# A perceiver layer on one core: the order of steps that share a stretch is reversed, and the last tiles' timetable is moved

## The chip, the cores and the metric

The kernel runs on one core of a Trainium2 chip. The time is the device time of one execution in microseconds (us); the number given for a kernel is the median of several runs. [...] An instruction that waits holds back everything behind it on its engine.

## The reference

All in float32. The layer has three parts, each with a layer norm ahead of it and a residual sum behind it:

```
x = x + cross_attention(norm(x), ctx, ctx)     # 32 x 64 queries, 32 x 1601 keys, 16 heads of 16
x = x + span_attention(norm(x))                # scores = -softplus(s1) * (pos - 64*sigmoid(s0))^2
x = x + ffn(norm(x))                           # (shared + experts / 2) / 2
shared  = (silu(x @ sw1 + sb1) * (x @ sw3 + sb3)) @ sw2 + sb2
experts = sum over k of gelu(x @ w1[e] + b1[e]) @ w2[e] + b2[e],  e = (11 * token + 7919 * k) % 8
```

The second part's attention runs over the 64 positions of one sequence, and its scores come from two numbers per head and position (s0, s1) alone. All softmaxes are exact ones.

## The kernel before

The 32 sequences are 16 **tiles** of two sequences (128 rows). The first part's attention is the bulk of the work: for each sequence and each half of the heads (64 "halves", `n`), keys and values are projected (`pk`, `pv`, L494), scores are made (`psc`, L548), DVE adds the mask (L572, L565) and keeps running maxima (`mrun`, L589), the maxima are turned over PE (`pm`, `pb`), POOL subtracts them (L620), ACT takes the exponential (L625), and PE multiplies with the values (`pvs`, L635).

A half is three **stretches** (3n, 3n+1, 3n+2). Beside it run short chains of small work, written as Python generators: `query_steps` makes the queries of the next tile (norm, `tr_q`, `pq` L465, `qbd` L473), `finish_steps` ends a sequence's first attention, and `span_steps(t)` does all of the second part for tile t and the norm of the third. Each `yield` names how many stretches later the chain goes on. `agenda` holds, for each stretch, the generators that are due, and `run(stretch)` takes each one step on, in list order, and appends it to the list of a later stretch. The program's order on PE, DVE, ACT and POOL is this written order: a `manual_schedule` keeps it.

The 23 steps of `span_steps` are, by place in the timetable `STEPS` (and the three other ones for the last tiles): 0 output projection `po` (L250), sum into x (L253) and statistics; 1 POOL's norm scalars (L205 to L208); 2 ACT's norm `xn_h` (L214); 3 transpose `tr_h`, copy `hT` (L262); 4 `psp` (L266), DVE `span`, `z` (L272, L273); 5 ACT `z` = exp (L280); 6 some 16 small DVE operations (L293 to L305); 7 POOL `sc` = pos - mean (L310); 8 ACT square (L314), POOL times soft (L315); 9 DVE `least` (L318); 10 to 13 four groups of four exponentials (L322); 14 `pval` (L334), copies `vbd` (L341); 15 DVE reciprocal (L346); 16 POOL weights `sc` (L348); 17 `psa`, copies `aT` (L356, L358); 18 `po2`, copy `o2T` (L366, L372); 19 `po3`, sum, statistics (L376, L379), and the transfer `x_kept` on SP (L381); 20 norm scalars; 21 `xn_f` (L214); 22 `tr_f` and the copies into `xfT` (L221, L389).

A tile's chain starts every 12 stretches and takes 24 to 25, so up to three tiles and a query chain meet in a stretch. Where "stretch 3 of a tile" is said, it is the stretch in which step 0 of that tile runs, counted as `STEPS` counts, modulo 12.

The last tiles (13, 14, 15) have their own timetables. After the last half (stretch 189 on) a loop over s = 2 to 21 calls `run(189 + s)`, then `gate()` as often as `gated` says, then starts the units that `begin` names. A **unit** u is one 128-channel slice of the shared network's hidden layer for a quarter of the tokens: one product with `sw1` and one with `sw3` (L664; for some units the second is made earlier, L672). `gate()` takes the oldest unit begun: ACT's Silu and DVE's product (L686, L687, or L691, L692). Units 12 to 15 need the third norm of tiles 12 to 15. All these products, and the small ones, take PSUM banks in turn from one pool of six (`mm_bank`). The last stage (L914 on) computes the experts and the output.

[...]

Of the kernel before, what the change touches and what calls it, by code (L numbers as in the profile page):

```python
# [89 lines left out]
def perceiver_kernel(ctx: ExitStack, tc: tile.TileContext, a: dict[str, bass.AP], out: bass.AP):  # L90
# [126 lines left out]
    def transposed(src, name: str):  # L217
# [12 lines left out]

    STEPS = (3, 4, 5, 6, 7, 8, 9, 11, 12, 15, 16, 17, 18, 19, 20, 20, 21, 22, 23, 24, 25, 26, 27)
    LAST_BUT_TWO = (
        3, 4, 5, 6, 7, 8, 9, 11, 12, 13, 13, 14, 15, 16, 17, 17, 17, 18, 20, 21, 22, 25, 27,
    )
    LAST_BUT_ONE = (
        2, 2, 3, 4, 5, 5, 6, 7, 8, 9, 10, 11, 12, 13, 14, 14, 14, 15, 16, 17, 17, 18, 19,
    )
    LAST = (2, 2, 3, 4, 5, 6, 8, 9, 10, 11, 12, 12, 12, 12, 13, 13, 13, 15, 16, 17, 17, 18, 19)
    SMALL = 6
# [343 lines left out]
    def maximum(n: int, k: int):  # L583

        dst = mrun
        if k == NKC - 1:
            dst = mxs[n] = work.tile([P, 4, P], F32, tag="mx", bufs=1, name="mx")
        dst, run = (m[:CHUNK].rearrange("p (r i) q -> p r i q", r=2) for m in (dst, mrun))
        nc.vector.tensor_tensor(dst, block_of(n, k), run, ALU.max)  # L589
# [105 lines left out]
    held_at: set = set()  # L695

    def run(stretch: int):
        for steps in agenda.pop(stretch, []):
            while (wait := next(steps, None)) == 0:
                pass  # L700
            if wait:
                agenda[stretch + wait].append(steps)
# [62 lines left out]
    for n, (b, c) in enumerate(halves[:-1]):  # L765
# [9 lines left out]
        def steps(g: int):  # L775
            run(3 * n + g)
            for u in extra.get(3 * n + g, ()):
                linear_factor(u)
# [14 lines left out]
        if not held:  # L793
            first_maxima(n + 1)
        run(3 * n)
        if n:
            values(n - 1, 1)
# [30 lines left out]
    stretch = 3 * last  # L828
# [17 lines left out]
    gate()  # L846


    begin = {4: (1, 2), 7: (7, 8, 5), 10: (9,), 12: (10,), 15: (6, 4), 19: (11,)}
    gated = {7: 2, 10: 2, 12: 1, 13: 1, 15: 1, 17: 2}  # L850
    for s in range(2, 22):
        run(stretch + s)
# [149 lines left out]
```

## Time and profile before

| | |
|---|---|
| median of 3 runs | 1526.94 us (1526.82 to 1529.74) |
| the profiled execution, its own time | 1529.89 us |
| its span, first to last instruction | 1528.1 us |
| steady loop, one tile | some 84 us (`po` at 643.4 and 727.7) |
| tail, last half to the experts' stage | 1374 to 1442 us |
| experts' stage | 1442 us to the end |

An engine's busy time is the time in which it had an instruction at work. In a timeline a line is a group of like instructions: start, time, engine, line and operation, tile written from tiles read, count, and in brackets the idle time ahead of it with what ended it. PE's line is 664 for units, and its clock, as granted, is in the windows view (1.00 is full speed).

### The profile page before, as it was taken

How to read it: one execution, taken by the hardware profiler on the slowest of the kernel's cores; microseconds unless marked ns; L12 is line 12 of the kernel's file. 1: busy time of each engine (PE TensorE's matmuls, PEld its weight loads, DVE VectorE, ACT ScalarE, POOL GpSimd, SP SyncE). 2: the span in 40 equal slices, each digit the busy share in tenths (PEclk: the TensorE clock that was granted, in tenths of full speed). 3: DMA queues.
4: the chain of work that ended last, by engine and by line, in shares of the span. 5: the costliest groups of instructions: out<-in, count | busy, mean ns of one | idle time of the engine just before them, and what ended most of it. 6: DMA issues, size and time to landing. Idle time of an engine off the chain costs nothing.

```text
span 1528.1 us, 62953 instructions
## 1 busy us (share of the span) xinstructions
PE 1470.4 (96%) x28600; PEld 1071.4 (70%) x28600; DVE 1222.8 (80%) x2332; ACT 947.7 (62%) x1727; POOL 1119.0 (73%) x508
## 2 busy tenths in 40 slices
PE   8999999999999999999999999999999999988999
PEld 5677767777777767777776767676777767654587
DVE  4889898988889898989888898888898889873100
ACT  3565657676667657676767666675767676756411
POOL 1777787888878887879878788878788787852610
PEclk9999999999999999999999999999999999999999
DMA  5111111111111101111111111111111111004100
GB/s 173 43 38 46 46 46 46 44 45 49 49 49 50 42 23 46 53 36 49 49 50 49 50 49 32 33 45 53 36 50 49 50 46 32 6 6 159 59 28 29
DMA packets 52076, 73.82 MB, mean 48 GB/s; under 512 B 3812, under 2 KB 51040, under 8 KB 51680
## 3 DMA queue, kind: packets, MB, share of 16 engines
q1 hardware_dynamic: 50992, 69.00, 14.7%
q8 instruction: 225, 3.69, 1.0%
q10 hardware_dynamic: 816, 0.79, 0.2%
q14 instruction: 43, 0.35, 0.1%
HBM read 65.57 MB, written 4.19 MB: 46 GB/s over the span
## 4 chain that ended last, share of the span: by engine, by line
PE 72%; DVE 17%; ACT 8%; issue 2%; POOL 0%; DMA 0%; ACTq 0%; DVEq 0%; POOLq 0%
PE pv L494 18%; PE pk L494 18%; PE psc L548 11%; PE pvs L635 8%; DVE mrun L589 7%; DVE prob L572 6%; PE py L932 4%; ACT sc L322 3%; PE pm L596 2%; ACT prob L625 2%; PE u L664 2%; PE ph L914 2%; PE pb L611 2%; PE pq L465 1%; PE psa L356 1%
## 5 line engine op out<-in xcount | busy, mean ns | idle before, releaser
L620 POOL TENSOR_TENSOR prob<-prob,mb 124x1664 f32<-124x1664 f32 x252 | 937.7, 3745 | 239.4 <-ACT mb L615 231.6
L572 DVE TENSOR_TENSOR prob<-psc,madd 124x512 f32<-124x512 f32 x768 | 506.6, 680 | 70.8 <-PE psc L548 69.2
L625 ACT ACTIVATE prob<-prob 124x1664 f32<-124x1664 f32 x256 | 406.9, 1590 | 181.7 <-POOL prob L620 179.1
L589 DVE TENSOR_TENSOR mrun<-prob,mrun 124x512 f32<-124x512 f32 x704 | 486.1, 691 | 40.7 <-ACT mrun L581 28.0
L494 PE MATMUL pk<-ct,wkT_sb 128*32 128x372 f32 (+1 forms) x2512 | 387.6, 489 | 5.7 <-DMA wkT_sb<-in_wkT 5.6
L494 PE MATMUL pv<-wvT_sb,ct 128*124 128x256 f32 x3524 | 380.9, 379 | 0.4 <-DVE prob L572 0.3
L494 PEld LDWEIGHTS pv<-wvT_sb,ct 128*124 128x124 f32 x3524 | 273.6, 132 | 108.7 <-issue 14.9
L548 PE MATMUL psc<-qbd,kT 32*124 32x128 f32 x6400 | 246.6, 280 | 17.0 <-ACT hT L262 9.7
L494 PEld LDWEIGHTS pk<-ct,wkT_sb 128*32 128x32 f32 (+1 forms) x2512 | 148.9, 127 | 135.9 <-issue 88.9
L548 PEld LDWEIGHTS psc<-qbd,kT 32*124 32x124 f32 x6400 | 204.7, 182 | 54.7 <-issue 19.7
L526 ACT COPY v<-pv 124x512 f32<-124x512 f32 (+1 forms) x224 | 124.4, 556 | 164.0 <-PE pv L494 163.9
L635 PE MATMUL pvs<-prob,v 124*17 124x64 f32 x13312 | 214.3, 220 | 1.2 <-issue 1.2
L635 PEld LDWEIGHTS pvs<-prob,v 124*17 124x17 f32 x13312 | 196.7, 98 | 23.1 <-issue 15.2
L509 ACT ACTIVATE kT<-pk,cols 128x372 f32<-128x372 f32 (+2 forms) x256 | 146.7, 585 | 69.1 <-PE pk L494 69.0
L322 ACT ACTIVATE sc<-sc,least 128x64 f32<-128x64 f32 x256 | 85.7, 339 | 2.8 <-DVE least L318 2.8
L934 DVE SCALAR_TENSOR_TENSOR ot<-py,prob 128x256 f32<-128x256 f32 x16 | 6.8, 424 | 75.7 <-PE py L932 75.7
L581 ACT COPY mrun<-prob 124x512 f32<-124x512 f32 x64 | 38.2, 597 | 41.4 <-DVE soft L305 38.3
L664 PE MATMUL u<-xfT,sw_sb 128*128 128x512 f32 x128 | 61.1, 627 | 0.9 <-ACT xfT L389 0.9
L596 PE MATMUL pm<-cst,mx 124*128 124x124 f32 x256 | 42.1, 285 | 17.0 <-DVE mx L589 14.1
L611 PEld LDWEIGHTS pb<-cst,mc 128*124 128x124 f32 x256 | 29.5, 135 | 36.8 <-DVE mc L603 28.9
L548 PE MATMUL pvs<-qbd,kT 32*124 32x128 f32 x256 | 54.9, 294 | 0.0
L565 DVE TENSOR_TENSOR prob<-psc,madd_fifth 124x256 f32<-124x256 f32 x64 | 27.0, 421 | 32.2 <-PE pvs L548 31.1
(126 smaller groups left out, 1242.4 us busy)
## 6 DMA issues: line engine op xcount, KB each, us to landing
ct<-in_ctxT SPq DMA_DIRECT2D x64, 372.0 KB, 3.2
ct<-in_ctxT SPq DMA_DIRECT2D x32, 496.0 KB, 5.1
ct<-in_ctxT SPq DMA_DIRECT2D x32, 361.0 KB, 4.0
w<-in_w SPq DMA_DIRECT2D x16, 256.0 KB, 7.0
x<-in_x SPq DMA_DIRECT2D x16, 128.0 KB, 2.1
x_kept<-x SPq DMA_DIRECT2D x16, 128.0 KB, 1.8
prob<-x_kept SPq DMA_DIRECT2D x8, 256.0 KB, 5.6
out<-ot SPq DMA_DIRECT2D x16, 128.0 KB, 1.9
```

The lines of the kernel that those rows point to most:

```text
L322: nc.scalar.activation(sc[:, h, :], sc[:, h, :], AF.Exp, bias=least[:, h : h + 1], scale=-1.0, accum_out=total[:, h : h + 1],)
L494: nc.tensor.matmul(out[at:end], lhsT=lhsT[:, at:end], rhs=rhs, start=start, stop=stop, **(dict(tile_position=(0, at)) if tiled else {}),)
L509: nc.scalar.activation(kTs[c][:, k0 : k0 + kn], ps[:, :kn], AF.Identity, bias=cols[:, B_K + c : B_K + c + 1])
L526: nc.scalar.copy(vs[b % 2][:kn, 2 * u : 2 * u + n, :, :DK], ps[:kn, : n * D].rearrange("p (n h d) -> p n h d", n=n, d=DK),)
L548: product = nc.tensor.matmul(ps[:CHUNK, at * P : (at + 1) * P], lhsT=kTs[c][32 * j : 32 * j + 32, k0 : k0 + CHUNK], rhs=qbd[b // 2][32 * j ...
L572: nc.vector.tensor_tensor(pair_of(n, j)[:, c0 : c0 + 4, :].rearrange("p k (e q) -> p k e q", e=2), pss[j][:CHUNK].rearrange("p (k e q) -> ...
L589: nc.vector.tensor_tensor(dst, block_of(n, k), run, ALU.max)
L596: nc.tensor.transpose(ps[:, j * CHUNK : (j + 1) * CHUNK], m[:CHUNK, j, :], ident[:CHUNK, :CHUNK])
L620: engine.tensor_tensor(sj, sj, m[:CHUNK, j, None, :].to_broadcast([CHUNK, NKC, P]), ALU.subtract)
L625: nc.scalar.activation(pair_of(n, j), pair_of(n, j), AF.Exp)
L635: nc.tensor.matmul(pvs[32 * j : 32 * j + DK + 1, c, :, r, :], lhsT=v[:kn, k, 8 * c + h, :], rhs=pair_of(n, h // 2)[:kn, k, (h % 2) * S : ( ...
L664: nc.tensor.matmul(ps, lhsT=w[:, c, hc * P : (hc + 1) * P], rhs=xfT[:, c, :, slot], start=(c == 0), stop=(c == 1),)
```

## The change

Four edits:

```diff
     LAST_BUT_TWO = (
-        3, 4, 5, 6, 7, 8, 9, 11, 12, 13, 13, 14, 15, 16, 17, 17, 17, 18, 20, 21, 22, 25, 27,
+        3, 4, 5, 6, 7, 8, 9, 11, 12, 13, 13, 14, 15, 16, 17, 17, 17, 18, 20, 21, 21, 21, 23,
     )
     LAST_BUT_ONE = (
-        2, 2, 3, 4, 5, 5, 6, 7, 8, 9, 10, 11, 12, 13, 14, 14, 14, 15, 16, 17, 17, 18, 19,
+        2, 2, 3, 4, 5, 5, 6, 7, 8, 9, 10, 10, 10, 10, 12, 12, 12, 13, 14, 15, 15, 16, 17,
     )
...
     def run(stretch: int):
-        for steps in agenda.pop(stretch, []):
+        for steps in reversed(agenda.pop(stretch, [])):
             while (wait := next(steps, None)) == 0:
                 pass
             if wait:
                 agenda[stretch + wait].append(steps)
...
-    begin = {4: (1, 2), 7: (7, 8, 5), 10: (9,), 12: (10,), 15: (6, 4), 19: (11,)}
+    begin = {3: (1, 2), 7: (7, 8, 5), 10: (9,), 12: (10,), 15: (6, 4), 19: (11,)}
```

`run` takes the generators of a stretch from the end of their list. Tile 13 does its norm scalars and `xn_f` in the stretch of `po3`, and its `tr_f` four stretches sooner. Tile 14 does its four groups of exponentials in one stretch, and everything after them two stretches sooner. Units 1 and 2 begin in s = 3 and not in s = 4. No instruction is added or taken away but table loads.

## The prediction

> **What bounds the kernel now.** I read the page's engine shares, then its chain by line, then the tail (1374 us to 1442 us) on the PE and ACT timelines, because the edits to the lists act only there, and last one tile of the steady loop, because `run` is used everywhere.
>
> ```profile
> PE 1470.4 (96%) x28600; PEld 1071.4 (70%) x28600; DVE 1222.8 (80%) x2332; ACT 947.7 (62%) x1727; POOL 1119.0 (73%) x508
> ```
>
> PE is the bound: 1528.1 - 1470.4 = 57.7 us idle in all, so whatever is won or lost is a PE gap. The tail, PE first:
>
> ```profile
> 1379.33 1.10 PE L250 MATMUL po<-woP_sb,oT 128*128 128x256 f32 x4 [1.59 <-DVE oT L718]
> ...
> 1387.61 1.09 PE L356 MATMUL psa<-cst,sc 128*128 128x128 f32 x8 [1.34 <-POOL sc L348]
> ...
> 1390.02 9.98 PE L664 MATMUL u<-xfT,sw_sb 128*128 128x512 f32 x20
> 1399.84 1.03 PE L376 MATMUL po<-woutT_sb,o2T 128*128 128x256 f32 x4
> 1404.02 0.44 PE L221 MATMUL tr_f<-cst,xn_f 128*128 128x128 f32 x2 [3.15 <-ACT xn_f L214]
> 1404.98 8.83 PE L664 MATMUL u<-xfT,sw_sb 128*128 128x512 f32 x16 [0.52 <-ACT xfT L389]
> ...
> 1419.50 1.09 PE L356 MATMUL psa<-cst,sc 128*128 128x128 f32 x8 [1.05 <-POOL sc L348]
> ```
>
> The last column is the gap before the group. Two gaps are waits of tile 14 (1.34, 3.15); the last (1.05) is tile 15, whose weighted `sc` is late. From there to the end tile 15 is the chain, and after 1427.90 PE works without a gap. ACT beside it:
>
> ```profile
> 1393.09 1.28 ACT L280 ACT_TABLE_LOAD   x1
> 1394.39 0.23 ACT L280 ACTIVATE z<-z 128x32 f32<-128x32 f32 x1
> ...
> 1404.49 0.43 ACT L389 COPY xfT<-tr_f 128x128 f32<-128x128 f32 x2 [0.53 <-PE tr_f L221]
> ```
>
> Tile 15's `z` exponential is done at 1394.62, but DVE reaches the small operations only at 1401.92, behind tile 14's sum.
>
> **The reversal in the steady loop.** A reversed list is appended to the next stretch in reversed order, and is reversed again there. So the order of the generators flips in every second stretch only. The built instruction order confirms it: per tile only its stretches 3, 5 and 7 change; POOL keeps its order.
>
> (a) Stretch 3 of a tile: `tr_f` goes ahead of `po`, `least` behind the norms. DVE then does stats_q (0.56 us), and waits for `po`, which is 0.31 us later; its L589 starts 0.6 us later. The cover is DVE's next wait for PE, 1.21 us, and the tightest PE wait on DVE in between (`pv` at 733.12 for the L565 that ends 732.35) has 0.77 us to spare. Cost 0; without the cover 14 x 0.6 = 8.4 us.
> (b) Stretch 5: the norms ahead of the four exponentials. Same instructions, norm scalars ready long before: 0.
> (c) Stretch 7:
>
> ```profile
> 757.79 0.53 PE L266 MATMUL psp<-wspanT_sb,hT 128*128 128x32 f32 x4
> 758.16 1.14 PE L465 MATMUL pq<-xnT,wqT_sb 128*128 128x128 f32 x8
> 759.23 1.15 PE L548 MATMUL psc<-qbd,kT 32*124 32x128 f32 x32
> 760.31 2.67 PE L494 MATMUL pk<-ct,wkT_sb 128*32 128x372 f32 x32
> ...
> 759.81 1.48 ACT L473 ACTIVATE qbd<-pq,bq,own 128x128 f32<-128x128 f32 x4
> ```
>
> `pq` now precedes `psp`, so the six-bank pool hands `pq`'s bank to the first tiled `pk` (L494) where `psp`'s bank stood before; the second `pk` used to get it. That `pk` now waits for the four `qbd` activations, at 760.31. They start 1.10 us after `pq` starts (89.67 to 90.77, where no exponential stands ahead): 757.79 + 1.10 + 1.50 = 760.39, plus 0.05 for the signal = 760.44. **Stall 0.13 us in each of 14 tiles = 1.8 us.** Bounds: 0.05 (the activations are seen as done earlier) to 0.2, so 0.7 to 2.8 us. Behind the waiting `pk` stand the other `pk` and `pv`; everything on PE shifts.
>
> **The tail, in times of the old profile.** Norm of tile 13: POOL has its scalar at 1375.60, so `xn_f` runs 1375.64; the sixteen exponentials start 1376.13 and take 5.31 (1411.71 to 1417.02) to 1381.44. Silu table and u3: 1381.46 + 1.30 = 1382.76, done 1383.45.
> - PE: after `pvs` (1377.64) `tr_f` 0.31, `pval` 1.01, u1 1.72 (four starts 0.43 apart): 1380.68. u2 stands in the bank of u3's first product, so it waits for that Silu until 1383.49. **Gap 2.7.**
> - DVE: the reciprocal now stands behind the gates of u3 and u0: 1384.74. POOL 1385.08 to 1386.98, `psa` 1387.04. **Gap 1.8.** All four exponential groups together win only 0.57 us here.
> - `po` of tile 15 stands behind `psa`: 1387.97 (before: 1379.33). Its norm passes DVE (1.24 after the matmul's start to the aggregate's end at 1390.21), POOL (1.30), ACT at 1391.55. On ACT `o2T` of tile 14 is queued behind that norm: 1392.04 to 1392.41. `po3` 1392.46. **Gap 2.5.**
> - `tr_h`, its copy, `psp`: u7 starts 1394.80. Five half units x 1.72 end at 1403.40; only then `tr_f` of tile 14 (POOL, `x_kept` and the rest of that norm are covered by these 8.6 us).
> - ACT takes the `xfT` copies of `tr_f` **ahead of** `z`: ready 1404.32, table 1.30, `z` at 1405.62 where it was 1394.39. The small operations follow at once: POOL starts `sc` at 1405.90 + 1.64 = 1407.54 (before 1403.56). Square 1409.48, product 1410.62, `least` 1412.55, exponentials 1413.80, and 7.79 as before (1411.71 to 1419.50) to `psa`: 1421.59.
>
> **Tile 15 ends 2.1 us later**, with the order behind it unchanged. u9's second half waits on the new timing of u7's Silu, but `psa` still comes last. Moving `begin` of u1, u2 to 3 buys nothing, since u2 waits.
>
> SP: `x_kept` of tile 14 is moved ahead of six weight loads, which wait with it until about 1394; their first use is after 1455, so 0.
>
> Hand-over to the last stage:
>
> ```profile
> 1440.22 0.69 ACT L691 ACTIVATE prob<-u,cols 128x512 f32<-128x512 f32 x1 [2.75 <-PE u L664]
> ...
> 1441.73 2.10 PE L914 MATMUL ph<-xfT,w 128*128 128x256 f32 x9
> 1442.01 0.75 DVE L692 SCALAR_TENSOR_TENSOR prob<-u,b3twice,prob 128x512 f32<-128x512 f32 x1 [2.68 <-PE u L664]
> ```
>
> The banks rotate differently: the first `ph` now gets the bank of u15's second product (before: u14's first), and waits for that L692, 1442.76 + 0.05. **1.1 us**; nothing covers it.
>
> [...]
>
> [...] Here the clock is halved after windows that were half idle:
>
> ```profile
> 1390.00:1392.00 2.00, 2.00 (x7) 0.95 (x4) 0.00 (x0) 1.82 (x3) 0.00 (x0) 0.50 1.10 348
> ...
> 1406.00:1408.00 2.00, 2.00 (x4) 0.85 (x3) 1.04 (x2) 1.99 (x4) 0.00 (x0) 0.50 0.00 0
> ```
>
> (The 0.50 is the granted clock.) [...] A half-rate stretch lasted 3.4 us and cost at most 1.7 us. I count two on the path: about 1.4 us near u7 (the old 1.2 us there is not in my 1403.40), and about 1.2 us at `psa` to u11, ahead of which PE now idles 3 to 4 us. Bounds 0 to 5; I take 2.6.
>
> **Sum.** 1.8 + 2.1 + 1.1 + 2.6 = +7.6 us. Against the profiled execution (span 1528.1, its own time 1529.9) that is 1537.5; that execution is 2.95 us above the median, near the top of the three runs. Against the median 1526.94 it is 1534.5; I say **1534 us**.
>
> **Rivals.**
> A. No extra half-rate stretch on the path (windows fall kindly): +5.0, 1532. For it: the tail has a 61% busy window (1419.6 to 1423) at full clock. Against: 6.3 us with u2 alone.
> B. The waits cascade: half rate twice in a row after `psa`, and 0.2 per tile: 1.8 + 1.0 + 2.1 + 1.1 + 5 = +11, 1538.
> C. Not slower: PE order decides, not tile 15. If `z` were not held by the copies of `tr_f` (had ACT taken it first), POOL's `sc` would start near 1400 and `psa` would find PE busy. The 1.05 gap and the old 3.15 + 0.52 then go, and the new gaps cost 2.7 + 1.8 + 2.5 + 0.5 against 1.59 + 0.58 + 1.34: -0.7; with hand-over and the loop's 1.8 at their low ends (0 and 0.7) it is 0, 1527. It decides as soon as `z` ends before about 1401. Against: both queues are in order, and the built order puts the copies first.
> D. The change does little of what it says: flips hidden, loop 0, tail +2.1 + 1.1, the clock as before: +3, 1530, at the edge of what counts.
>
> **Chances.** Forecast 0.5, A 0.2, B 0.12, D 0.1, C 0.08. A difference of 0.2% (3.1 us) is about what this kernel's runs can tell from none. Slower by more: all of forecast, A, B and half of D, 0.87; within: half of D and most of C, 0.09; faster 0.04. Range 1529.5 to 1538.5: D's edge to B.
>
> **What would show it.** The `z` exponential behind the `xfT` copies, 11 us later; u2 waiting on L691; `po3` waiting on `o2T`; `psa` of tile 15 2 to 5 us later; a 1.1 us gap before the first L914; 14 gaps before L494 on L473; six table loads after 1374 us instead of eight. I am wrong if PE's idle time after 1374 us is below the old 10 us, or if tile 15's `psa` isn't late.

## The result, and the profile after

The changed kernel takes 1543.4 us (median of 4: 1539.34 to 1546.07) beside 1527.78 us (four runs) for the kernel before: ratio 1.0098, 95% interval 1.0073 to 1.0124. A second set gave 1540.6 us (six runs) against 1529.55 us (27 runs of the kernel before, 1526.32 to 1535.32): 1.0076 (1.0058 to 1.0093), which is 11.6 us. It is slower, as forecast, but by 11.6 us (second set) to 15 us (first set) and not by 7.6, and both times lie above the range, which ends at 1538.5.

The page, PE's row (PE makes the matrix products and PEld loads their weights; DVE and POOL do vector work, ACT activations). PE's idle time is 62.1 us of the span of 1537.5, 4.4 more than before; its busy time grew by 5.0 with the same 28600 products.

```profile
PE 1475.4 (96%) x28600; PEld 1072.2 (70%) x28600; DVE 1222.6 (80%) x2332; ACT 946.1 (62%) x1725; POOL 1118.9 (73%) x508
```

The PE timeline of the tail (start, time, group; in brackets the gap ahead and what ended it):

```profile
1362.02 1.06 PE L596 MATMUL pm<-cst,mx 124*128 124x124 f32 x4 [2.43 <-DVE mx L589]
...
1383.29 1.99 PE L664 MATMUL u<-xfT,sw_sb 128*128 128x512 f32 x4 [2.12 <-ACT prob L691]
1386.89 1.09 PE L356 MATMUL psa<-cst,sc 128*128 128x128 f32 x8 [1.61 <-POOL sc L348]
1387.82 1.03 PE L250 MATMUL po<-woP_sb,oT 128*128 128x256 f32 x4
...
1392.25 1.74 PE L376 MATMUL po<-woutT_sb,o2T 128*128 128x256 f32 x4 [2.83 <-ACT o2T L372]
...
1395.76 10.66 PE L664 MATMUL u<-xfT,sw_sb 128*128 128x512 f32 x20
...
1410.70 5.42 PE L664 MATMUL u<-xfT,sw_sb 128*128 128x512 f32 x12 [1.56 <-ACT prob L691]
...
1424.40 1.97 PE L356 MATMUL psa<-cst,sc 128*128 128x128 f32 x8 [3.64 <-POOL sc L348]
...
1451.06 7.17 PE L914 MATMUL ph<-xfT,w 128*128 128x256 f32 x32 [0.91 <-DVE prob L692]
```

The three predicted waits are there: u2 on the Silu (2.12; forecast 2.7), psa on POOL (1.61; 1.8), po3 on `o2T` (2.83; 2.5). Tile 15's psa is 4.9 us later than before, behind a gap of 3.64. The same group of eight takes 1.97 here, where the granted clock is 0.50, and 1.09 at 1386.89, where it is 1.00. ACT:

```profile
1406.68 0.43 ACT L389 COPY xfT<-tr_f 128x128 f32<-128x128 f32 x2 [8.49 <-PE tr_f L221]
1407.13 1.28 ACT L280 ACT_TABLE_LOAD   x1
1408.42 0.23 ACT L280 ACTIVATE z<-z 128x32 f32<-128x32 f32 x1
```

`z` stands behind the copies, 14 us later than before; ACT has two table loads fewer (1725 instructions, not 1727). In both profiles a load of 1.28 us stands at each turn from Exp to Silu, from Silu to Exp and, once, from Silu to Gelu: after 1374 us eight before, six here. Last, PE's clock in windows that follow the boundaries of the clock itself (window, its length, busy time of PE, PEld, DVE, ACT, POOL, then the granted clock):

```profile
1419.95:1423.36 3.41, 0.81 (x2) 0.00 (x0) 0.25 (x1) 3.38 (x16) 0.91 (x1) 1.00 0.00 0
1423.36:1426.77 3.41, 2.37 (x24) 1.98 (x24) 0.75 (x1) 2.23 (x4) 0.99 (x1) 0.50 0.00 0
1426.77:1430.19 3.42, 2.54 (x28) 1.84 (x21) 1.29 (x2) 1.66 (x4) 0.00 (x0) 0.50 0.00 0
1430.19:1433.60 3.41, 3.41 (x5) 1.43 (x5) 1.03 (x3) 0.53 (x1) 1.62 (x5) 0.50 0.11 38
```

PE works 0.81 of 3.41 us, and three windows follow at half clock: the first two of them have gaps again (1.04 and 0.88 us idle), and only behind the third, which is busy throughout, does the clock come back. From the last half to the last units the clock is halved for 23.9 us (1361.9 to 1368.7, 1392.6 to 1399.5, 1423.4 to 1433.6); before it was 13.7 us.

In this execution the steady loop nets nothing: the last half's pm starts at 1362.02, and in the profile before:

```profile
1362.03 1.06 PE L596 MATMUL pm<-cst,mx 124*128 124x124 f32 x4 [2.43 <-DVE mx L589]
...
1441.73 7.07 PE L914 MATMUL ph<-xfT,w 128*128 128x256 f32 x32
```

So the whole difference of this pair, 9.3 us, lies between the last pm and the first ph (89.04 us; before 79.70). Two things were open: whether the loop's 1.8 us exist, and what the times have beyond the sum.

### The profile page after: what moved, and what is told of

Read it like the earlier page. It is cut to its first block, busy times and chain, and to the rows that moved or that the text cites. A ratio compares the mean times of both kernels' runs of the same rounds, so it can differ in the third digit from the quotient of the medians.

```text
span 1537.5 us, 62954 instructions
## 1 busy us (share of the span) xinstructions
PE 1475.4 (96%) x28600; PEld 1072.2 (70%) x28600; DVE 1222.6 (80%) x2332; ACT 946.1 (62%) x1725; POOL 1118.9 (73%) x508
## 4 chain that ended last, share of the span: by engine, by line
PE 70%; DVE 17%; ACT 9%; issue 2%; POOL 1%; DMA 0%; DVEq 0%; POOLq 0%; ACTq 0%
PE pv L494 18%; PE pk L494 18%; PE psc L548 10%; PE pvs L635 8%; DVE mrun L589 7%; DVE prob L572 6%; PE py L932 4%; ACT sc L322 3%; ACT prob L625 2%; PE u L664 2%; PE pm L596 2%; PE ph L914 2%; PE pb L611 1%; ACT qbd L473 1%; PE po L376 1%
```

## The experiments

Two theories at first. T: the loop pays about what was forecast, and what the sum lacks is half-rate clock in the tail. L: it lies in the loop. Times are medians beside the kernel before in the same set (1528.4 to 1530.1); the ratio is what counts.

**The whole and its two halves.** `again` is the changed kernel. `loop_only` is the old kernel with `agenda.pop(stretch, [])[:: -1 if stretch < 178 else 1]`; `tail_only` is the changed one with `>= 178`.

> The changed kernel once more, for a second profile and more times. Theory T (tail and clock): times spread over 1539 to 1546 again; the last half's pm (L596) starts at about 1362 as before, within 0.7 us, so the loop nets nothing; what an execution has over the +9.4 us of the first profile is more half-rate clock after 1370 us, in steps of 3.4 us at up to 1.7 us lost each. Rival L (loop): the last half's pm starts 3 to 6 us later than 1362 in a slow execution, with the clock after 1370 as in the first profile.

> The old timetables and the old begin; lists reversed only before stretch 178, so that the tail has its old order and 13 tiles of the loop have the new one. My prediction's term: 13 x 0.13 = +1.7 us, 1529.5. Theory T: 0 to +1.7 us, 1527.5 to 1529.5. Rival L: +4 to +7 us, 1532 to 1535.

> The changed kernel with lists reversed only from stretch 178 on, so that the steady loop has its old order. Theory T: nearly all of the loss stays, +12 to +16 us, 1540 to 1544. Rival L: +8 to +10 us, 1536 to 1538.

| | us | ratio (95%) | x 1528.6 us |
|---|---|---|---|
| again | 1540.6 | 1.0076 (1.0058 to 1.0093) | +11.6 |
| loop_only | 1531.61 | 1.0016 (1.0007 to 1.0025) | +2.4 |
| tail_only | 1537.44 | 1.0056 (1.0036 to 1.0076) | +8.6 |

The halves add up to 11.0. L falls; T's loop is at its upper end or a little over. The waits view of `again` for PE (who waited for what: us in all, times, longest) has the forecast wait, in 14 tiles:

```profile
PE pk L494 <- ACT qbd L473: 2.2, 14, 0.2
```

0.16 us each where 0.13 was forecast. `loop_only` has it too (2.2 us, 14 times); no run takes this one wait away alone. A single pair of profiles could not show it: from the second pm to the last but one, seven executions with the old list order in the loop took 1277.6 to 1280.4 us (median 1278.4), thirteen with the reversed one 1279.8 to 1286.4 (1281.5). The first pair were 1279.79 and 1279.77, one high in its group and the other the lowest.

**Swaps in the tail.** One list taken in its old order turns all later ones too, so the tail can be undone from its end: `[:: 1 if stretch == 3 * last + 8 else -1]` (z_first), with 5 (o2T_first) and 4 (po_first) for the 8; `plain_order` has no reversal at all.

> The changed kernel with one swap on ACT: at s = 8 tile 15's z exponential stands ahead of tile 14's xfT copies; nothing else moves. Theory T (z held by the copies makes tile 15 late): z runs at about 1397 instead of 1408, psa of tile 15 finds PE still busy, its 3.6 us gap and the half-rate stretch behind it go: 5 to 9 us less than the changed kernel, 1534 to 1538. Rival P (PE's order and the waits of tile 14 make the loss, tile 15 has slack): at most 2 us less, 1541 to 1543.

> The changed kernel with the list of s = 5 alone taken in its old order, which turns all later stretches of the tail too: on ACT o2T of tile 14 ahead of xn_h of tile 15 and z ahead of the xfT copies, on PE tr_h of tile 15 ahead of po3 of tile 14; psa of tile 14 still ahead of po of tile 15. By the traces tr_h then starts at about 1392.5 and not 1393.8: 1.2 us less than with z alone first, 1536.5 to 1537. If the 2.8 us gap ahead of po3 is paid in full: 2.8 us less, 1535.

> The same with the list of s = 4 in its old order: also po of tile 15 ahead of psa of tile 14 on PE, so that it runs in the gap in which psa waits for POOL, and tile 15's norm starts 2.7 us sooner. The steady loop stays reversed. If this one place of po holds most of the loss: the old-order kernel plus the loop's cost, 1529.5 to 1530.5. If the loss is spread evenly over the swaps: 1533 to 1535.

> The new timetables and the new begin, lists in their old order. Theory T (timetable and reversal share the loss): the loop's 1.8 us and z's hold (2.6 us by the swap) go, u2's, psa's and po3's waits stay: 1535 to 1537. Rival R (the reversal makes the loss, the timetables alone gain): 1526 to 1530.

| | us | ratio (95%) | from the one above |
|---|---|---|---|
| again | 1540.6 | 1.0076 | |
| z_first | 1538.0 | 1.0053 (1.0033 to 1.0073) | -3.5 |
| o2T_first | 1533.65 | 1.0036 (1.0024 to 1.0049) | -2.6 |
| po_first | 1531.19 | 1.0015 (1.0004 to 1.0026) | -3.2 |
| plain_order | 1527.35 | 0.9987 (0.9980 to 0.9995) | -4.3 |

(The last column is the difference of the ratios times 1528.6 us; neighbours' intervals overlap, the ends are clear.) The last step has the loop's 2.4 us in it. No single swap holds the loss; `o2T_first` came out 3 us lower than its traces promised, `po_first` 1 us higher. The swap of z was worth 3.5 us where 5 to 9 were expected, and ACT of `z_first` says why:

```profile
1399.37 0.23 ACT L280 ACTIVATE z<-z 128x32 f32<-128x32 f32 x1
1407.32 0.43 ACT L389 COPY xfT<-tr_f 128x128 f32<-128x128 f32 x2 [7.72 <-PE tr_f L221]
1407.77 1.28 ACT L691 ACT_TABLE_LOAD   x1
1409.07 1.27 ACT L691 ACTIVATE prob<-u,cols 128x512 f32<-128x512 f32 x2
1410.22 1.05 ACT L314 ACTIVATE sc<-sc 128x1024 f32<-128x1024 f32 x1
```

`z` is 9 us earlier, but the square of the same chain (L314) stands behind the same copies and the two Silus after them: it is 2.06 us earlier (1412.28 in the changed kernel), and psa with it. PE still waits 2.47 us for that psa. (This execution, 1533.94 us, is the fastest of its six, and no half rate follows psa in it.) Without any reversal the new timetables are 2.0 us faster than the kernel before (interval 0.8 to 3.1).

**The clock alone.** Products that nobody reads keep PE at work in its gaps:

```diff
+    def filler(n: int):
+        for _ in range(n):
+            nc.tensor.matmul(spare_pvs, lhsT=ident, rhs=woP[:, 0, :], start=True, stop=True)
...
+        filler({14: 6, 15: 1}.get(t, 0))
         for c in range(2):
             nc.tensor.matmul(
                 po3[:, :D], lhsT=o2T[:, c, :], rhs=woutT[:, c, :], start=(c == 0), stop=(c == 1)
```

> The kernel before, with products that nobody reads put into PE's gaps from the last half on (10 ahead of and behind pm, then 5, 4, 11, 3 and 3 ahead of po of tile 15, psa of tile 14, tr_f of tile 14, psa and po3 of tile 15; each 0.26 us at full clock, just under the gap in sum). Theory T (short PE gaps halve the clock, and that is paid in time): no half-rate stretch after 1360 us, 3 to 5 us less than before, 1525 to 1526.5 against 1529.6. Rival N (the half rate falls where PE would wait anyway): within 1 us of before.

> The changed kernel, filled in the same way (7 ahead of u2, 5 ahead of psa of tile 14, 10 ahead of its po3, 5 ahead of u9's second product, 11 and 2 ahead of psa and po3 of tile 15, 10 around the last pm). Theory T (what my sum lacks is half-rate clock): no half-rate stretch after 1360 us, 6 to 9 us less than the changed kernel, 1532 to 1535; and against the filled kernel before the waits alone stay, +5 us as in my sum without its clock term (1.8 + 2.1 + 1.1), at most +7. Rival W (the waits of the tail were sized too small): +9 to +11 us against the filled kernel before.

> The kernel before, filled again, with about half of the filling: a product stands twice in the profile, so that one is 0.45 us and the first filling overran several gaps. Now 5 and 1 around the last pm, then 1, 2, 6, 2, 2 (po of tile 15, psa of tile 14, tr_f of tile 14, psa and po3 of tile 15): 0.9 to 2.6 us, each below its gap. Theory T (the half rate is paid in time): clock 1.00, 1525 to 1526.5. Rival N (it falls where PE waits anyway): 1528 to 1529.5.

> The changed kernel with half of the filling: 5 and 1 around the last pm, 6 ahead of u2, 3 and 6 ahead of psa and po3 of tile 14, 3 ahead of u9's second product, 7 and 1 ahead of psa and po3 of tile 15. Clock 1.00. If the half rate is paid in time: 5 us below the changed kernel, 1535 to 1536. Against the filled kernel before, theory T (my sum's waits were right, its clock too small): +5 to +6; rival W (the waits were too small, the clock about right): +9 to +10.

The first pair was filled to overflowing (22 records, 4.91 us, in a gap of 3.15), so its times, 1529.52 (ratio 1.0005) and 1539.22 (1.0065), hold the overrun too. The second pair fits: 1527.23 us, 0.9994 (0.9985 to 1.0004), and 1534.04 us, 1.0038 (1.0026 to 1.0051). `after_fill2` around tile 15's psa (its lines are shifted by the inserted ones; L660 is the filler):

```profile
1414.64 3.70 PE L671 MATMUL u<-xfT,sw_sb 128*128 128x512 f32 x8
1418.18 3.18 PE L660 MATMUL pvs<-woP_sb,cst 128*128 128x256 f32 x14
1421.98 1.09 PE L357 MATMUL psa<-cst,sc 128*128 128x128 f32 x8 [0.62 <-POOL sc L348]
```

psa takes 1.09 again, and the clock is 1.00 to the experts' stage. The changed kernel gains 0.0038 of its ratio by it, 5.8 us (2.5 to 9.1, the two intervals taken together); the kernel before 0.9 us, not told from nothing, and its profile still has a stretch of 6.8 us at half rate. What is left between the two filled kernels, 0.0044 or 6.7 us (4.3 to 9.1), is waits; the other 4.9 of the 11.6 us are clock. That lies between T and W, and the times alone are too wide to part the two.

The profiles part them, since the stretch from the last pm to the first ph holds the tail without the loop. `after_fill2` has these marks beside the lines above:

```profile
1363.54 0.61 PE L598 MATMUL pm<-cst,mx 124*128 124x124 f32 x4
...
1387.52 1.09 PE L357 MATMUL psa<-cst,sc 128*128 128x128 f32 x8 [0.32 <-POOL sc L348]
...
1445.30 7.17 PE L923 MATMUL ph<-xfT,w 128*128 128x256 f32 x32 [0.91 <-DVE prob L699]
```

| us from start to start | before | changed | `again` | `after_fill2` |
|---|---|---|---|---|
| last pm to psa of tile 14 | | 24.87 | 24.00 | 23.98 |
| psa of tile 14 to psa of tile 15 | | 37.51 | 37.51 | 34.46 |
| last pm to psa of tile 15 | 57.47 | 62.38 | 61.51 | 58.44 |
| psa of tile 15 to the first ph | 22.23 | 26.66 | 26.44 | 23.32 |
| last pm to the first ph | 79.70 | 89.04 | 87.95 | 81.76 |

So filling takes 6.2 us (against `again`) to 7.3 us (against the first profile) off the changed kernel's tail. In the kernel before it takes at most 0.5 (79.17 in `before_fill`, 80.03 in `before_fill2`). Most of what the tail lost is clock.

**Which gaps.**

> The changed kernel with only the gaps around the last pm filled (5 and 1 products), which both kernels share. If the half-rate losses add up: the stretch of 3.4 to 6.8 us behind pm goes, 1 to 1.5 us less than the changed kernel, 1539 to 1539.5; the stretches behind 1380 us stay. If they cascade, so that PE reaches the next gap sooner and waits there: no change, 1540.6.

> Only the gaps ahead of u2, psa and po3 of tile 14 filled (6, 3, 6). This prices the term near u7, 1.4 us in my sum. Adding up: 2 to 2.5 us less, 1538 to 1538.5, and the five half units from u7 on take 8.8 us in the profile. Cascade: under 1 us.

> Only the gaps ahead of u9's second product, psa and po3 of tile 15 filled (3, 7, 1). This prices the term from psa to u11, 1.2 us in my sum. Adding up: 2.5 to 3 us less, 1537.5 to 1538, psa to the last units as short as with all gaps filled (21.98 to 30.38: 8.4 us). Cascade: under 1 us.

1543.45 us (1.0094, 1.0081 to 1.0107), 1538.28 (1.0067, 1.0053 to 1.0080) and 1540.02 (1.0067, 1.0052 to 1.0081): against `again` the first is 2.8 us slower and the others are 1.4 us faster, and their intervals overlap that of `again`. The profiles show each filling's gain where it was made. `fill_tile14`:

```profile
1388.74 1.09 PE L357 MATMUL psa<-cst,sc 128*128 128x128 f32 x8 [0.29 <-POOL sc L348]
...
1396.39 8.83 PE L671 MATMUL u<-xfT,sw_sb 128*128 128x512 f32 x20
...
1423.20 1.97 PE L357 MATMUL psa<-cst,sc 128*128 128x128 f32 x8 [3.64 <-POOL sc L348]
```

From psa to psa it takes 34.46 us, as with all gaps filled, and 3.05 less than the changed kernel; the units from u7 on take 8.83, as expected. `fill_tile15`:

```profile
1429.55 1.09 PE L357 MATMUL psa<-cst,sc 128*128 128x128 f32 x8 [0.62 <-POOL sc L348]
...
1452.86 7.17 PE L921 MATMUL ph<-xfT,w 128*128 128x256 f32 x32 [0.91 <-DVE prob L699]
```

From psa to ph it takes 23.31 us, 3.1 less than `again` and 3.35 less than the first profile. These two places together make the 6.2 us.

The filling of `fill_pm` gained nothing up to psa of tile 14 (23.97 us beside 24.00 in `again`):

```profile
1389.59 3.23 PE L668 MATMUL u<-xfT,sw_sb 128*128 128x512 f32 x4 [3.73 <-ACT prob L695]
...
1401.42 11.72 PE L668 MATMUL u<-xfT,sw_sb 128*128 128x512 f32 x20
```

PE came to u2 sooner and waited longer, 3.73 us and not 2.12, with half rate right behind it and again from u7 on (11.72 where 8.83 is full clock). In the profiled executions the extra time does not come from the tail, which is 1.9 us shorter than in `again` from pm to ph (86.05). It comes from the loop, which the filling leaves alone: in `fill_pm` it took 1286.4 us, the longest of the thirteen, with two stretches of 3.4 us at half rate (`fill_tile15`: 1284.9). Why the loop ran longer there stays open.

**Hand-over and begin.** `ph_banks` opens `ps_h` ahead of `ps_y`; `after_begin4` and `plain_begin4` put `begin` back to `{4: (1, 2), ...}` in the changed and in the old-order kernel.

> The changed kernel with the two PSUM pools of the last stage opened in the other order, so that the first ph takes a bank that units 14 and 15 do not hold. Theory T: the 0.9 us gap ahead of the first L914 goes, and nothing takes its place: 0.9 to 1.1 us less, 1539.6. Rival H (Gelu's table load or the first weights are next in line): the gap stays or moves to the first py, 1540.6.

> The changed kernel with the old begin: units 1 and 2 behind psa of tile 14 and po of tile 15, ahead of po2. If moving them bought nothing (my prediction): 1540 to 1542. By the traces the four half units (3.6 us) then fill the 2.8 us gap ahead of po3, but push po2 and so o2T back to about 1393.2, 1 us later than now, and leave PE idle for 7 us ahead of psa, two windows at half rate: 1 to 3 us more, 1541.5 to 1544.

> The old-order kernel with the old begin. If begin buys nothing: 1527 to 1527.5. By the traces po of tile 15 then starts right behind its oT, some 4 us sooner, but tr_h stands behind units 1 and 2 at about 1389.7 where it was 1387.8: 1 to 2 us more, 1528.5 to 1529.5.

In `ph_banks` the first ph follows without a gap:

```profile
1438.62 14.00 PE L664 MATMUL u<-xfT,sw_sb 128*128 128x512 f32 x32 [0.35 <-ACT xfT L389]
1452.46 7.07 PE L914 MATMUL ph<-xfT,w 128*128 128x256 f32 x32
```

13.84 us from the last units to ph, in the changed kernel 14.92 (1436.14 to 1451.06): 1.08 us less. Its time, 1540.43 (1.0075, 1.0054 to 1.0096), is too wide to show it. `after_begin4`: 1540.22 (1.0071, 1.0055 to 1.0087), not told from the changed kernel. `plain_begin4`: 1531.07 (1.0005, 0.9997 to 1.0014), so in the old order the earlier begin is worth 2.8 us (0.0018), all of what the new timetables and begin gain together: with units 1 and 2 behind psa PE stands idle for 8.00 us ahead of it.

**The version to keep**: the new timetables and begin, no reversal, gaps filled.

> The new timetables and begin in the old order, its gaps filled (5 and 1 around the last pm, 6 ahead of u2, 5 and 2 ahead of psa and po3 of tile 15). Clock 1.00 to the end, 2 us below the old-order kernel: 1525 to 1525.5, 3 to 4 us below the kernel before, ratio 0.9975. If the half rate costs nothing in that kernel, whose PE waits for tile 15 at psa in any case: 1527.

1525.18 us, ratio 0.9977 (0.9967 to 0.9986): 3.5 us faster than the kernel before, clock 1.00 in the tail.

## Why the prediction went wrong, step by step

| step | forecast, us | measured, us |
|---|---|---|
| loop, pk behind qbd | 1.8 | 2.4 (1.1 to 3.8) in time, the wait itself 2.2; nothing in the first pair |
| tail's waits, to psa of tile 15 | 2.1 | 1.9 by the profiles |
| hand-over, ph behind L692 | 1.1 | 1.1 by the profiles, not seen in time |
| half-rate clock | 2.6 | 6.2 to 6.4 by the profiles, 5.8 (2.5 to 9.1) in time |
| sum | 7.6 | 11.6 to 11.8; the whole, second set: 11.6 |

**The step that failed is the clock term.** It says "I count two on the path", about 1.4 near u7 and 1.2 from psa to u11, with bounds of 0 to 5. Half clock behind half-idle windows was right: PE was busy for 0.58 of 3.41 us (1389.23 to 1392.64) ahead of the first place and for 0.81 ahead of the second. The size was not. The term was added to tail times worked out at full clock behind psa of tile 14, so it stands against what the filling takes from the changed kernel at these two places: 3.05 us for the 1.4, and 3.1 to 3.35 for the 1.2. Each place was priced as one window of 3.4 us that costs at most 1.7 us. In the profile they are two and three windows long, with gaps inside all the slow windows but the last: around tr_h and psp behind 1392.6 (PE is busy for 2.95 us of the first slow window), and around po2 and po3 behind 1423.4 (2.37 and 2.54 us). That is rival B's cascade (+5 for the clock), to which I gave 0.12; its sum was +11. "A half-rate stretch lasted 3.4 us" was also a misreading of the profile before: the stretch behind the last pm holds two windows there, with gaps in the first (windows view of the kernel before, as above):

```profile
1361.61:1365.02 3.41, 2.22 (x16) 1.53 (x20) 0.95 (x2) 0.00 (x0) 0.00 (x0) 0.50 0.00 0
1365.02:1368.44 3.42, 3.42 (x105) 3.10 (x103) 2.48 (x2) 1.14 (x2) 0.00 (x0) 0.50 0.03 7
```

**The tail's waits were right.** Every wait named was there. The forecast had 59.56 us from the last pm to tile 15's psa (1421.59 less 1362.03), with the old half rate behind pm kept and full clock after psa of tile 14. Put together in the same way, the profiles give 24.87 + 34.46 = 59.33, which is 1.9 more than before (57.47). The part at full clock, psa of tile 14 to psa of tile 15, had been forecast at 34.55. With both kernels filled, the difference is no larger (58.44 beside 56.72 in `before_fill` and 57.80 in `before_fill2`). With the hand-over's 1.1 and the clock's 6.4 the tail's 9.3 us of the first pair are accounted for.

**The base.** The sum was set on 1526.94, the median of three, and not on the profiled execution's 1529.9, which I called near the top; 27 runs later gave 1529.55. So 2.6 us of the distance from 1534 to the second set's 1540.6 are the base and 4.0 the sum. The first set lies another 2.8 us higher in its median; only its lowest execution has a profile, so this part stays open.

**Rival C** (not slower if z is not held) falls by `z_first`, still 1.0053 with z first: the square behind the copies holds tile 15, whatever z does. What makes the kernel not slower is the old order as a whole. **That begin buys nothing** holds in the reversed kernel; the reason, u2's wait, isn't the whole one, since the same wait stands in the old order (2.83 in its profile), where begin is worth 2.8 us.

The sum has no term for the two table loads fewer; no run here separates what they gave.

## What to carry to other kernels

Turning a list of pending steps puts work that is ready behind work that waits, on every in-order engine at once; look at what each waiting instruction now has behind it, all the way down the same chain (the square as well as z). Price a PE gap by the clock too: here the gaps went on behind 1392.6 and 1423.4, half clock lasted 6.83 and 10.24 us, and the cost was that of the whole stretch and not of the first gap. Take differences of whole kernels from many runs, or from the one segment that changed: the three single fillings could not be told apart in time, and were plain from psa to psa. Compare like clock with like clock.

## What the runs showed of the hardware

In the profiles of the kernel before and of the changed one, the granted clock was halved for 6.83, 3.41 and 3.41 us (from 1361.61, 1388.92 and 1405.99) and for 6.83, 6.83 and 10.24 us (from 1361.92, 1392.64 and 1423.36) between 11 and 1500 us, one to three windows of 3.41 us each time. PE's busy time in such windows (at half clock with products at their slow length), and the clock in the window that followed:

| clock | profile | followed by half clock | followed by full clock |
|---|---|---|---|
| full | before | 1.40, 1.75 and 1.45 us (from 1358.20, 1385.51, 1402.57) | 1.71 (1399.16), 1.83 (1040.76) and all above 1.9 |
| full | changed | 1.08, 0.58 and 0.81 us (from 1358.51, 1389.23, 1419.95) | none below 1.9 |
| half | before | 2.22 us | all three of 3.41 us |
| half | changed | 2.37, 2.54, 2.54 and 2.95 us | all three of 3.41 us |

So half clock followed 1.75 us busy and full clock 1.71 and 1.83. The 1.66 us of idle time behind 1385.51 were two gaps (0.58, in part, and 1.34 us); ahead of 1392.64 it was one, of 2.83 us.

Products to no use paid here: the changed kernel ran 5.8 us sooner with work added. Too many of them cost it again: with 50 and not 32, as in the first filling, the clock was 1.00 to the experts' stage as well, but the gain was 1.7 us (1.0065 beside 1.0076), not told from nothing.
